# A two-layer graph network: stores issued later than their producers, and the last four norms on VectorE

## The chip, the cores and the metric

The kernel runs on one core of one Trainium2 chip. The metric is the time of one execution on the device in microseconds (us), as the median of several runs. TensorE (PE in the profile) multiplies matrices, with its weight loads listed apart as PEld; VectorE is DVE, ScalarE is ACT, GpSimd is POOL, and SyncE is SP. In this kernel SP issues nearly all transfers between HBM and the on-chip memory SBUF, one after the other.

## The reference

128 batches of a 128 x 512 array x go through two layers, in f32. H is 8 heads, and adj is a 128 x 128 matrix that serves as the mixing matrix of layer 0 and as the attention mask of layer 1.

```python
# layer 0
h = jnp.maximum(_layernorm(x), 0.0)
x = x + (einsum('nm,bmd->bnd', adj, h) @ weight + bias)
# layer 1
h = jnp.maximum(_layernorm(x), 0.0)
q, k, v = heads(h @ w_qkv)
attn = softmax(where(adj == 0, -inf, q @ k.T * scale))
o = (attn @ v) @ w_proj + b_proj
ln = (o - mu) * rsqrt(var + 1e-5) * gamma + beta      # mu, var over the 512 values of a row
x = x + o + ln
```

The change touches the place of many stores in the order of work, and the last three lines for the last four batches.

## The kernel before

The kernel writes its own schedule. While it is built, `put(t, f, *a)` places a piece of work at a planned time t in us in a heap, and the pieces are then emitted in order of t. Each engine runs its own instructions in that order, and each instruction waits on semaphores for what it depends on. So the planned time sets only the order on each engine. SP is one such stream: a transfer that waits for its data holds back all transfers behind it.

```python
    def put(t, f, *a):
        count[0] += 1
        heapq.heappush(later, (t, count[0], f, a))
    ...
    while later:
        t, _, f, a = heapq.heappop(later)
        f(*a)
```

Two transposes are made by a round trip through HBM[...]: `exchange` stores an array to HBM and brings it back with four loads in another order. It serves the normalized input h1 of layer 1 (in the profile d<-h and h<-d) and the softmax probabilities (d<-s and sx<-d). In line numbers, L220 is the store and L225 the loads.

```python
    def exchange(t, b, dst=None):
        w = b.shape[2]
        d = dram.tile([P, Q, w], F32, name=f"d{w}")
        nc.sync.dma_start(out=d, in_=b)                                  # L220
        put(t, exchange_back, b if dst is None else dst, d)

    def exchange_back(dst, d):
        for q in range(Q):
            nc.sync.dma_start(out=dst[q * R:(q + 1) * R, :, :],          # L225
                              in_=d[:, q, :].rearrange("(n r) w -> r n w", n=Q))
```

The result of layer 0 is parked in HBM (x1d) until the end of the batch, and loaded again as x1b (or x, in the last eight batches).

```python
    def keep_x1(i):
        if i >= AHEAD:
            nc.gpsimd.tensor_tensor(X[i], X[i], beta_b, op=ALU.add)      # L335
        X1D[i] = dram.tile([P, D], F32, name="x1d", bufs=20)
        nc.sync.dma_start(out=X1D[i], in_=X.pop(i))                      # L337
```

The softmax of a batch: VectorE adds the mask to the scores (L401) and takes the maximum (L406), ScalarE computes the exponentials (L425), GpSimd divides by the sum (L435). Then comes the exchange, and VectorE transposes the returned blocks (L441) for the attention's matmuls (L450). There are two buffers s for the masked scores and one buffer sx for what returns. Late odd batches (123, 125, 127) have `spare` buffers: the two halves of one free h1T tile, half 0 for the scores and half 1 for what returns.

```python
    def softmax_mask(i, ps):
        s = late(0) if spare(i) else work.tile([P, Q, H * R], F32, name="s", bufs=2)
        ...
            nc.vector.tensor_tensor(s[...], ps[e]..., m4, op=ALU.add)    # L401

    def softmax_divide(i, t, e, sm):
        nc.vector.reciprocal(sm, sm)                                     # L433
        ...
        nc.gpsimd.tensor_tensor(e, e, sm..., op=ALU.mult)                # L435
        S[i] = late(1) if spare(i) else work.tile([P, Q, H * R], F32, name="sx", bufs=1)
        exchange(max(t + 5, read_at(i)), e.rearrange(...), S[i])
```

Products with weights add their parts into PSUM banks; VectorE adds a bank to the result in SBUF (L306 for the first part, L263 for later ones, with pd, pc and pz as the banks), and TensorE reuses the bank after that. For the last four batches the projection is a plain product (L468), and VectorE adds the bias (L663).

The last norm is split over three engines. VectorE computes mean and variance (L201, L202, L204), GpSimd the power -1/2 (L206), VectorE the shift (L211), GpSimd adds o to x1 (L485), ScalarE normalizes (L490), GpSimd multiplies by gamma (L491) and adds (L497; L496 adds beta in the first eight batches only, as the others have it in x1 already). SP stores the output (L498).

```python
    def finish(batches, t):
        shifts, args = stats_of([O[i] for i in batches])
        put(t + 3, shifts)
        for n, (i, arg) in enumerate(zip(batches, args)):
            put(t + 1 + 3 * n, lambda i=i: nc.gpsimd.tensor_tensor(X1B[i], X1B[i], O[i], op=ALU.add))  # L485
            put(t + 3 + 3 * n, finish_out, i, t + 3 + 3 * n, arg)

    def finish_out(i, t, arg):
        n = O.pop(i)
        nc.scalar.activation(n, n, AF.Identity, **arg)                                                 # L490
        put(t + 1.5, lambda: nc.gpsimd.tensor_tensor(n, n, gamma_b, op=ALU.mult))                      # L491
        put(t + 3, finish_last, i, n, X1B.pop(i))

    def finish_last(i, n, x1):
        if i < AHEAD:
            nc.gpsimd.tensor_tensor(n, n, beta_b, op=ALU.add)                                          # L496
        nc.gpsimd.tensor_tensor(n, n, x1, op=ALU.add)                                                  # L497
        nc.sync.dma_start(out=out[i], in_=n)                                                           # L498
```

The constants that matter are AHEAD = 8 (the first batches, with another order), LATE = 120 (the last eight batches, which form the tail with an order of its own) and LAST = 124.

Of the kernel before, what the change touches and what calls it, by code (L numbers as in the profile page):

```python
# [20 lines left out]
def kernel(  # L21
# [30 lines left out]
    nc = tc.nc  # L52
    B, N, D = x.shape
    H = 8
    HD = D // H
    C = D // P
    G = 4
    Q, R = 4, 32
# [5 lines left out]
    work = ctx.enter_context(tc.tile_pool(name="work", bufs=2))  # L64
    stat = ctx.enter_context(tc.tile_pool(name="stat", bufs=8))
# [5 lines left out]
    LATER = []  # L71
    X, H0, YT, X1D, H1, H1T, WQ, QKT, V, S, PT, OT, O, X1B, LEFT0, LEFT1, LEFT2 = ({} for _ in range(17))
# [15 lines left out]
    gamma_b = const.tile([P, D], F32)  # L88
# [74 lines left out]
    minus_half = const.tile([P, 2], F32)  # L163
# [48 lines left out]

        return shifts, [dict(bias=shift[:, n:n + 1], scale=rs[:, n:n + 1]) for n in range(w)]

    def exchange(t, b, dst=None):


        w = b.shape[2]
        d = dram.tile([P, Q, w], F32, name=f"d{w}")
        nc.sync.dma_start(out=d, in_=b)  # L220
        put(t, exchange_back, b if dst is None else dst, d)

    def exchange_back(dst, d):
        for q in range(Q):
# [100 lines left out]
    def norm1_out(i, t, arg):  # L325
        h1 = H1[i] = work.tile([P, Q, C, R], F32, name="h1", bufs=4)
        nc.scalar.activation(h1.rearrange("p q c r -> p c q r"), X[i].rearrange("p (c q r) -> p c q r", c=C, q=Q),
                             AF.Relu, **arg)
        exchange(t + 4.5, h1.rearrange("p q c r -> p q (c r)"))
        put(t + (1.5 if i >= AHEAD else 0), keep_x1, i)  # L330

    def keep_x1(i):

        if i >= AHEAD:
            nc.gpsimd.tensor_tensor(X[i], X[i], beta_b, op=ALU.add)  # L335
        X1D[i] = dram.tile([P, D], F32, name="x1d", bufs=20)
        nc.sync.dma_start(out=X1D[i], in_=X.pop(i))  # L337


    def flip(i):  # L340
# [53 lines left out]
        put(t + 1, softmax_mask, i, ps)  # L394

    def softmax_mask(i, ps):
        s = late(0) if spare(i) else work.tile([P, Q, H * R], F32, name="s", bufs=2)
        s = s.rearrange("p q (h r) -> p h q r", h=H)
        m4 = maskb.rearrange("p (q r) -> p q r", q=Q).unsqueeze(1).to_broadcast([P, C, Q, R])
        for e in range(2):  # L400
            nc.vector.tensor_tensor(s[:, e * C:(e + 1) * C], ps[e].rearrange("p c (q r) -> p c q r", q=Q), m4, op=ALU.add)  # L401
        put(softmax_at(i), softmax_max, i, softmax_at(i), s)
# [6 lines left out]
    def spare(i):  # L409
        return i > LATE + 2 and i % 2  # L410

    def late(n):

        if not LATER:
            t = work.tile([P, C, G, P], F32, name="h1T").rearrange("p (n c) j m -> p n (c j m)", n=2)
            LATER.extend(t[:, n].rearrange("p (q w) -> p q w", q=Q) for n in range(2))
        return LATER[n]

    def softmax_exp(i, t, s, shift):
# [12 lines left out]
    def softmax_divide(i, t, e, sm):  # L432
        nc.vector.reciprocal(sm, sm)  # L433
        e = e.rearrange("p h q r -> p q h r")
        nc.gpsimd.tensor_tensor(e, e, sm.unsqueeze(1).unsqueeze(3).to_broadcast([P, Q, H, R]), op=ALU.mult)  # L435
        S[i] = late(1) if spare(i) else work.tile([P, Q, H * R], F32, name="sx", bufs=1)
        exchange(max(t + 5, read_at(i)), e.rearrange("p q h r -> p q (h r)"), S[i])

    def flip_probs(i):
        PT[i] = work.tile([P, 2 * C, P], F32, name="pT", bufs=2)  # L440
# [44 lines left out]
            put(t + 1 + 3 * n, lambda i=i: nc.gpsimd.tensor_tensor(X1B[i], X1B[i], O[i], op=ALU.add))  # L485
            put(t + 3 + 3 * n, finish_out, i, t + 3 + 3 * n, arg)

    def finish_out(i, t, arg):
        n = O.pop(i)
        nc.scalar.activation(n, n, AF.Identity, **arg)  # L490
        put(t + 1.5, lambda: nc.gpsimd.tensor_tensor(n, n, gamma_b, op=ALU.mult))  # L491
        put(t + 3, finish_last, i, n, X1B.pop(i))

    def finish_last(i, n, x1):
        if i < AHEAD:
            nc.gpsimd.tensor_tensor(n, n, beta_b, op=ALU.add)  # L496
        nc.gpsimd.tensor_tensor(n, n, x1, op=ALU.add)  # L497
        nc.sync.dma_start(out=out[i], in_=n)  # L498

# [8 lines left out]
    BEGIN, LAST, AHEAD = -3, B - G, 8  # L508
# [36 lines left out]
    LATE = LAST - G  # L545
    AT = {key: [] for key in "asQpD"}
    t, last = when(LATE, 0), ""
# [39 lines left out]
    for j in range(B // 2):  # L587
        a, b = 2 * j, 2 * j + 1
        i = a - 8
        if a < AHEAD:  # L590
            t = mix_at(a) - (8.5 if a else 5)
            put(t, norm0, j, t)
            for n in (a, b):
                t = mix_at(n) + 5.2
# [15 lines left out]
        i = a + 5  # L610
        t = attend_at(b) + 2
        if b < LAST:
            put(t, pair_left, j, t, 3.4 if i < LATE else 1.5, OT, LEFT2, "osum")
            n = 7 * (a - LATE + 4) // 2
# [3 lines left out]
        else:  # L618
            ends = []
            for n in (a, b):  # L620
                t = AT["D"][n - LAST]
                put(t, project_whole, n, t)
                ends.append(((n,), t + 4.6))
        for batches, t in ends:
            for n in batches:
                put(t - 7 + 3 * (n % 2), reload, n)
            put(t, finish, batches, t)

    steps = []
# [63 lines left out]
```

## Time and profile before

| What | Value |
| --- | --- |
| median of 3 runs (lowest to highest) | 2372.13 us (2368.23 to 2372.77) |
| span of the profiled execution | 2374.6 us |
| mean granted TensorE clock | 0.996 |
| moved by DMA | 518.86 MB, 218 GB/s in the mean |
| start of the tail (attention of batch 116) | 2243.1 us |
| last matmul ends | 2361.8 us |

The profile shows one execution. For each engine it gives the busy time and its share of the span, and for groups of equal instructions the line, the output and inputs, the count and the mean duration. The waits name the engine and line that waited, and the instruction whose end released it. The chain of waits is followed back from the last instruction, so it shows what each step waited for. The timeline lists single instructions with their start and duration, and in brackets the idle time before them. SPq lines are transfers being issued on SP; they take effect some microseconds later (a store d<-s of 512 KB lands 3.0 us after its issue in the median, a load sx<-d of 128 KB as well).

### The profile page before, as it was taken

Reading aid. Unit: us, or ns where it says so; the run is one execution under the profiler, and the core shown is the slowest. Engines: PE = TensorE matmul, PEld = TensorE weight load, DVE = VectorE, ACT = ScalarE, POOL = GpSimd, SP = SyncE. Lnnn points to the kernel's source line nnn. Section 1 sums busy time; section 2 is a strip of 40 time slices with the busy share of each in tenths; the row PEclk is TensorE's granted clock in tenths of the full one; section 3 lists DMA queues with packets and bytes.
Section 4 is the critical chain, followed back from the end, with each engine's and each line's share of the span. In section 5 each row is a group of like instructions: output and inputs, shape, how many; then the busy total and the mean of one; then the engine's idle time right before and its main releaser. Section 6 shows DMA issues by size and latency. Waiting matters only on the chain.

```text
span 2374.6 us, 43019 instructions
## 1 busy us (share of the span) xinstructions
PE 2332.3 (98%) x14131; PEld 2052.9 (86%) x14131; DVE 1462.2 (62%) x3287; ACT 1066.1 (45%) x3202; POOL 1671.4 (70%) x1592
## 2 busy tenths in 40 slices
PE   8999999999999999999999999999999999999996
PEld 7888888888888888888888888888888888888885
DVE  6556656665665566666666665666666666566654
ACT  3444444454444444444544444444445444444442
POOL 4467777777677766776776777677777767866667
PEclk9999999999999999999999999999999999999998
DMA  7576676766766767677677767677676676676664
GB/s 261 186 221 204 220 231 214 232 222 211 227 218 215 225 211 231 217 220 235 214 216 233 218 217 229 215 227 222 218 232 216 217 233 213 222 229 208 213 209 139
DMA packets 395885, 518.86 MB, mean 218 GB/s; under 512 B 39696, under 2 KB 247696, under 8 KB 395664
## 3 DMA queue, kind: packets, MB, share of 16 engines
q1 hardware_dynamic: 394976, 515.53, 68.7%
q8 instruction: 113, 1.85, 0.3%
q14 instruction: 108, 0.88, 0.1%
q10 hardware_dynamic: 688, 0.59, 0.1%
HBM read 345.05 MB, written 170.92 MB: 217 GB/s over the span
## 4 chain that ended last, share of the span: by engine, by line
PE 83%; DMA 4%; POOL 4%; DVE 4%; ACT 2%; SPq 2%; issue 1%; POOLq 0%; DVEq 0%
PE pc L372 36%; PE pd L300 24%; PE pz L372 6%; PE ps L392 4%; PE pmix L286 4%; PE po L450 4%; PE pz L300 4%; DMA sx<-d 2%; SPq L225 2%; DMA x1b<-x1d 1%; ACT s L425 1%; PE pd L468 1%; POOL x1b L485 1%; DVE pT L441 1%; DVE st L201 1%
## 5 line engine op out<-in xcount | busy, mean ns | idle before, releaser
L206 POOL TENSOR_TENSOR rs<-ve,minus_half 128x2 f32<-128x2 f32 (+1 forms) x194 | 135.6, 699 | 618.0 <-DVE ve L204 617.3
L372 PE MATMUL pc<-hsum,wq 128*128 128x256 f32 x1984 | 468.3, 379 | 3.4 <-POOL o L491 1.8
L372 PEld LDWEIGHTS pc<-hsum,wq 128*128 128x128 f32 x1984 | 376.6, 190 | 55.4 <-POOL o L491 2.2
L425 ACT ACTIVATE s<-s,mx 128x128 f32<-128x128 f32 x1000 | 387.8, 389 | 4.2
L435 POOL TENSOR_TENSOR s<-s,sm 128x1024 f32<-128x1024 f32 x125 | 239.1, 1913 | 38.4 <-DVE sm L433 38.2
L300 PE MATMUL pd<-wp_sb,osum 128*128 128x256 f32 x992 | 254.2, 379 | 1.4 <-DVE sm L433 1.4
L300 PE MATMUL pd<-w_sb,ysum 128*128 128x256 f32 x960 | 246.3, 379 | 0.0
L663 ACT COPY oT<-po 128x512 f32<-128x512 f32 x128 | 74.9, 586 | 372.0 <-PE po L450 372.0
L372 PE MATMUL pc<-wq,hsum 128*128 128x256 f32 x992 | 238.1, 383 | 1.0 <-ACT s L425 1.0
L372 PE MATMUL pc<-h1T,wq 128*128 128x256 f32 x992 | 237.6, 382 | 0.0
L441 DVE STREAM_TRANSPOSE pT<-sx 128x1024 f32<-128x1024 f32 x125 | 155.0, 1240 | 125.0 <-DMA sx<-d 123.0
L372 PEld LDWEIGHTS pc<-wq,hsum 128*128 128x128 f32 x992 | 186.6, 190 | 29.3 <-ACT s L425 1.3
L372 PEld LDWEIGHTS pc<-h1T,wq 128*128 128x128 f32 x992 | 185.9, 190 | 27.9 <-DMA wq<-in_L_gnn_w_qkv_dram 0.3
L306 DVE TENSOR_TENSOR o<-pd,bp_b 128x256 f32<-128x256 f32 x248 | 103.0, 416 | 171.7 <-PE pd L300 171.4
L300 PEld LDWEIGHTS pd<-wp_sb,osum 128*128 128x128 f32 x992 | 184.0, 190 | 24.5 <-issue 1.8
L376 ACT COPY qkT<-pc 128x512 f32<-128x512 f32 x256 | 144.5, 575 | 128.6 <-PE pc L372 128.4
L300 PEld LDWEIGHTS pd<-w_sb,ysum 128*128 128x128 f32 x960 | 177.9, 190 | 21.7
L490 ACT ACTIVATE o<-o,shift,rs 128x512 f32<-128x512 f32 x128 | 103.4, 808 | 196.4 <-POOL osum L234 123.0
L401 DVE TENSOR_TENSOR s<-ps,maskb 128x512 f32<-128x512 f32 x250 | 155.4, 683 | 56.4 <-PE ps L392 55.6
L425 ACT ACTIVATION_READ_ACCUMULATOR s<-s,mx 128x1 f32 x1000 | 187.2, 187 | 0.0
L201 DVE BATCH_NORM_STATS2 st<-x 128x6 f32<-128x512 f32 x256 | 171.9, 672 | 4.4 <-DMA x<-in_x_dram 4.4
L485 POOL TENSOR_TENSOR x1b<-x1b,o 128x512 f32<-128x512 f32 x120 | 152.9, 1275 | 25.7 <-DMA x1b<-x1d 25.2
(141 smaller groups left out, 4691.8 us busy)
## 6 DMA issues: line engine op xcount, KB each, us to landing
wq<-wt SPq DMA_DIRECT2D x372, 256.0 KB, 4.0
wq<-in_L_gnn_w_qkv_dram SPq DMA_DIRECT2D x279, 256.0 KB, 3.7
d<-s SPq DMA_DIRECT2D x125, 512.0 KB, 3.0
sx<-d SPq DMA_DIRECT2D x500, 128.0 KB, 3.0
x<-in_x_dram SPq DMA_DIRECT2D x128, 256.0 KB, 4.5
d<-h SPq DMA_DIRECT2D x128, 256.0 KB, 2.9
x1d<-x SPq DMA_DIRECT2D x128, 256.0 KB, 3.1
h<-d SPq DMA_DIRECT2D x512, 64.0 KB, 2.3
```

Of the source, the lines that this page charges most:

```text
L201: nc.vector.bn_stats(st, src)
L206: nc.gpsimd.tensor_tensor(rs, ve, minus_half[:, :w], op=ALU.pow)
L300: nc.tensor.matmul(p[:, 0, :], lhsT=left[k][:, c, :], rhs=w_sb[:, k, c, :], start=first and c == 0, stop=last and c == 1, skip_group_check ...
L306: nc.vector.tensor_tensor(results[n], p[:, 0, :], addend[n // 2][:, n % 2 * F:(n % 2 + 1) * F], op=ALU.add)
L372: nc.tensor.matmul(p[:, half, :], lhsT=lhsT, rhs=rhs, start=first and half == 0 and c == 0, stop=last and c == 1, skip_group_check=True)
L376: nc.scalar.copy(results[n], p)
L401: nc.vector.tensor_tensor(s[:, e * C:(e + 1) * C], ps[e].rearrange("p c (q r) -> p c q r", q=Q), m4, op=ALU.add)
L425: nc.scalar.activation(s[:, h], s[:, h], AF.Exp, bias=shift[:, h:h + 1], scale=scale, accum_out=sm[:, h:h + 1])
L435: nc.gpsimd.tensor_tensor(e, e, sm.unsqueeze(1).unsqueeze(3).to_broadcast([P, Q, H, R]), op=ALU.mult)
L441: nc.vector.transpose(PT[i].rearrange("p h (q r) -> p q h r", q=Q), S.pop(i).rearrange("p q (h r) -> p q h r", h=H))
L485: put(t + 1 + 3 * n, lambda i=i: nc.gpsimd.tensor_tensor(X1B[i], X1B[i], O[i], op=ALU.add))
L490: nc.scalar.activation(n, n, AF.Identity, **arg)
```

## The change

The aim is that no transfer at the head of SP's stream waits for its producer, and that the last batches leave less work on GpSimd. It has four parts.

- Each store gets its own planned time, some us after the instruction that makes its data: 1.2 us for h1, 2.2 us for the probabilities, 2 us for x1 (where GpSimd still adds beta), 5 us for an output of a batch under 120 and 1.5 us for the others. The loads that bring exchanged data back keep their planned times.
- The store of an x1 without beta and the other stores become pieces of work of their own, so other transfers can be placed between.
- The spare buffers alternate: batch 125 has its scores in one of two free yT tiles and batch 127 in the other, and what returns for them goes to the two halves of the h1T tile.
- For batches 124 to 127 the last norm ends with two VectorE operations, each of which reads two tensors and one value per row: (o - mean) * gamma, then that times the power plus x1. ScalarE's activation, the shift and two GpSimd operations fall away for them.

```diff
-    def exchange(t, b, dst=None):
+    def exchange(t, t_back, b, dst=None):
         w = b.shape[2]
         d = dram.tile([P, Q, w], F32, name=f"d{w}")
-        nc.sync.dma_start(out=d, in_=b)
-        put(t, exchange_back, b if dst is None else dst, d)
+        put(t, nc.sync.dma_start, d, b)
+        put(t_back, exchange_back, b if dst is None else dst, d)
 ...
-        exchange(t + 4.5, h1.rearrange("p q c r -> p q (c r)"))
-        put(t + (1.5 if i >= AHEAD else 0), keep_x1, i)
+        exchange(t + 1.2, t + 4.5, h1.rearrange("p q c r -> p q (c r)"))
+        t += 1.5 if i >= AHEAD else 0
+        put(t, keep_x1, i, t)
 ...
-        nc.sync.dma_start(out=X1D[i], in_=X.pop(i))
+        put(t + (2 if i >= AHEAD else 0), nc.sync.dma_start, X1D[i], X.pop(i))
 ...
-        s = late(0) if spare(i) else work.tile([P, Q, H * R], F32, name="s", bufs=2)
+        s = late((i - LATE - 1) // 2 * (i > LATE + 3)) if spare(i) else work.tile([P, Q, H * R], F32, name="s", bufs=2)
 ...
+        if n > 1 and len(LATER) == 2:
+            LATER.extend(work.tile([P, C, 2, P], F32, name="yT").rearrange("p c j m -> p c (j m)") for _ in range(2))
         return LATER[n]
 ...
-        S[i] = late(1) if spare(i) else work.tile([P, Q, H * R], F32, name="sx", bufs=1)
-        exchange(max(t + 5, read_at(i)), e.rearrange("p q h r -> p q (h r)"), S[i])
+        S[i] = late((i - LATE - 1) // 2 % 2) if spare(i) else work.tile([P, Q, H * R], F32, name="sx", bufs=1)
+        exchange(t + 2.2, max(t + 5, read_at(i)), e.rearrange("p q h r -> p q (h r)"), S[i])
 ...
+    def finish_end(i, t):
+        nc.gpsimd.tensor_tensor(X1B[i], X1B[i], O[i], op=ALU.add)
+        st = stat.tile([P, nc.vector.BN_STATS_DIM], F32, name="st")
+        nc.vector.bn_stats(st, O[i])
+        ...  # mean and variance mv, ve = variance + EPS
+        nc.gpsimd.tensor_tensor(rs, ve, minus_half[:, :1], op=ALU.pow)
+        n = work.tile([P, D], F32, name="h0", bufs=2)
+        nc.vector.scalar_tensor_tensor(n, O.pop(i), mv[:, 0:1], gamma_b, op0=ALU.subtract, op1=ALU.mult)
+        put(t + 1.9, end_last, i, n, rs)
+
+    def end_last(i, n, rs):
+        nc.vector.scalar_tensor_tensor(n, n, rs, X1B.pop(i), op0=ALU.mult, op1=ALU.add)
+        nc.sync.dma_start(out=out[i], in_=n)
 ...
-        put(t + 3, finish_last, i, n, X1B.pop(i))
+        put(t + 3, finish_last, i, t + 3, n, X1B.pop(i))
 ...
-        nc.sync.dma_start(out=out[i], in_=n)
+        put(t + (5 if i < LATE else 1.5), nc.sync.dma_start, out[i], n)
 ...
-            put(t, finish, batches, t)
+            if a < LAST:
+                put(t, finish, batches, t)
+            else:
+                put(t, finish_end, batches[0], t)
```

More of the change, by code (lines that the diff above doesn't have):

```diff
@@ L328, in norm1_out, with keep_x1 @@
                              AF.Relu, **arg)
-        exchange(t + 4.5, h1.rearrange("p q c r -> p q (c r)"))
-        put(t + (1.5 if i >= AHEAD else 0), keep_x1, i)
-    def keep_x1(i):
+        exchange(t + 1.2, t + 4.5, h1.rearrange("p q c r -> p q (c r)"))
+        t += 1.5 if i >= AHEAD else 0
+        put(t, keep_x1, i, t)
+    def keep_x1(i, t):
         if i >= AHEAD:
@@ L486, in finish @@
             put(t + 3 + 3 * n, finish_out, i, t + 3 + 3 * n, arg)
+    def finish_end(i, t):
+        nc.gpsimd.tensor_tensor(X1B[i], X1B[i], O[i], op=ALU.add)
+        st = stat.tile([P, nc.vector.BN_STATS_DIM], F32, name="st")
+        nc.vector.bn_stats(st, O[i])
+        mv = stat.tile([P, 2, nc.vector.BN_AGGR_DIM], F32, name="mv")[:, 0]
+        nc.vector.bn_aggr(mv, st)
+        ve = stat.tile([P, 2], F32, name="ve")[:, :1]
+        nc.vector.tensor_scalar(ve, mv[:, 1:2], EPS, None, op0=ALU.add)
+        rs = stat.tile([P, 2], F32, name="rs")[:, :1]
+        nc.gpsimd.tensor_tensor(rs, ve, minus_half[:, :1], op=ALU.pow)
[5 more added lines that the diff above has]
+        nc.sync.dma_start(out=out[i], in_=n)
     def finish_out(i, t, arg):
@@ L491, in finish_out, with finish_last @@
         put(t + 1.5, lambda: nc.gpsimd.tensor_tensor(n, n, gamma_b, op=ALU.mult))
-        put(t + 3, finish_last, i, n, X1B.pop(i))
-    def finish_last(i, n, x1):
+        put(t + 3, finish_last, i, t + 3, n, X1B.pop(i))
+    def finish_last(i, t, n, x1):
         if i < AHEAD:
```

## The prediction

> **What bounds the kernel now.** I read the engines' shares first, then the waits of TensorE, then those of the DMA queue (SP), then the chain of work into one of TensorE's gaps, and last the timeline of the end.
>
> ```profile
> PE 2332.3 (98%) x14131; PEld 2052.9 (86%) x14131; DVE 1462.2 (62%) x3287; ACT 1066.1 (45%) x3202; POOL 1671.4 (70%) x1592
> ```
>
> TensorE is the bound: 2374.6 - 2332.3 leaves 42.3 us in which it is not busy, and no matmul is removed or reordered (the order of instructions on TensorE is the same in both kernels). The change can only win some of these 42.3 us and the slow matmuls that follow a long gap. So which wait ends each gap? Columns of the waits: total us, times, longest.
>
> ```profile
> PE pd L300 <- DVE x L263: 9.9, 11, 1.9
> PE po L450 <- DVE pT L441: 3.5, 1, 3.5
> PE pd L300 <- DVE o L263: 3.4, 1, 3.4
> ...
> PE pc L372 <- POOL o L491: 1.8, 1, 1.8
> PE pd L300 <- DVE sm L433: 1.4, 1, 1.4
> ```
>
> By window, the first line lies wholly between 100 and 2243 us (4.5 up to 700, 3.7 up to 1400, 1.8 after): it is the steady part. The four others lie after 2243, in the tail. After the last matmul (2361.8 us) another 12.8 us pass. The DMA queue waits far longer, and in order:
>
> ```profile
> SPq L498 <- POOL o L497: 304.8, 123, 8.2
> SPq L220 <- POOL s L435: 225.9, 123, 21.7
> ```
>
> L498 is the store of an output, L220 the store of a batch's probabilities. What such a wait does to others shows in the chain into the 1.81 us gap at 304.76 (start, us, what):
>
> ```profile
> 295.82 1.28 POOL o L497
> 297.12 0.34 SPq L498
> ...
> 297.88 0.32 SPq L225
> ...
> 299.22 3.25 DMA sx<-d
> ...
> 302.55 1.25 DVE pT L441
> 303.80 0.58 DVE v L263
> 304.38 0.34 DVE x L263
> 304.76 1.13 PE pd L300 x4
> ```
>
> The load of sx (probabilities coming back, L225) sits in the SP stream behind an output store, which waits for GpSimd's last addition. The load starts late, VectorE stands 4.33 us before the transpose, and the addition that frees TensorE's PSUM bank is late. I looked at the gaps at 230, 590, 741, 814, 888, 1540 and 2191 too: in each one the output store is issued right after a GpSimd L497 and the sx load 0.4 us later.
>
> **What the Trainium skill says.** *Perfetto Trace Analysis*, section Sequencer Loop: an engine reads instructions one by one and each waits for its semaphores. The trace agrees for SP: nothing behind L498 is issued while it waits (at most 8.2 us). *SBUF — State Buffer*, Who interferes with whom: a VectorE instruction with two SBUF inputs and a GpSimd instruction that reads SBUF exclude each other for the whole instruction. The trace agrees: a VectorE subtraction of two SBUF tensors took 1.54 us at 31.71 while GpSimd added until 32.70, and 0.64 to 0.69 alone. *Vector Engine (DVE) Microarchitecture Reference*, Points that are easy to get wrong: a scalar-tensor-tensor with two non-bf16 SBUF sources runs at half throughput. No such instruction is in this trace. *TensorE: Matmul & The Clock Gate*, What's actually happening: TensorE's clock falls after an idle window of about 3.4 us. The trace agrees: after the 3.4 us gap the next four matmuls take 2.07 us, not 1.03, and the following eight 2.38, not 1.89.
>
> **The change part by part.**
>
> *Output stores 5 us later (batches under 120).* In the order of SP's instructions the odd batch's four sx loads and the weight load after them now stand ahead of the output store. What then holds the sx load is the weight load before it and the previous transpose, since there is one sx buffer. At 2182.64 the output store ended its wait and the sx load came at 2183.07; the weight load before was out at 2177.76 and the transpose ended at 2180.28 (2179.04 + 1.23). So the load moves from 2183.07 to about 2180.3, 2.8 us. In the same way it moves from 297.88 to about 292.6 (transpose 291.28 + 1.24), 5.3 us, and from 879.68 to about 876.4, 3.2 us. The longest gaps are 1.9, 1.8 and 1.7 us, each below its shift. **9.9 us go, and 0.1 each[...] (1.13 us for four matmuls, not 1.03): together 10 us**, with 8 to 11 as my range.
>
> *h1, probability and x1 stores 1 to 2 us later.* They wait less at the head of the queue. In some places a weight load, which itself waits for TensorE, now stands ahead of them (0.57 us at 1442.68). The returns h<-d start after x1d in both kernels. I give it 0, plus or minus 1 us. In the first 100 us TensorE's gaps come from GpSimd and ScalarE, whose order does not change: 0.
>
> *Other buffers for the masked scores of batches 125 and 127.* Before, all odd late batches share one half of an h1T tile:
>
> ```profile
> 2321.83 1.29 DVE L401 TENSOR_TENSOR h1T<-ps,maskb 128x512 f32<-128x512 f32 x2 [4.89 <-DMA d<-h1T]
> 2324.63 2.07 PE L300 MATMUL pd<-wp_sb,oT 128*128 128x256 f32 x4 [3.40 <-DVE o L263]
> ```
>
> The mask of 127 waits 4.89 us until the probabilities of 125 are stored, VectorE stands, and TensorE loses 3.40 us plus 1.04 and 0.49 of slow matmuls. With its own buffer the mask follows its scores, some 4.3 us sooner (2317.5). I then walk the order of VectorE: the transpose of 124 needs its load (issued until 2318.03, landing some 3.6 us later: 2321.7, not 2324.8), so the maximum of 127 comes at about 2323.7 and not 2327.08, 3.4 us sooner. The rest of 127 (exponentials, division, store, load, transpose) keeps that lead. In SP's new order one output store stands ahead of 127's store, which costs about 1.6 us there, but the load of 127 formerly stood behind the same two output stores (issued 2342.14, though its data was stored at about 2340.5), so its lead at the load is still 3.5. TensorE now arrives earlier too, and waits for this transpose again: the 3.5 us gap at 2348.66 stays, perhaps 4.8 long. **3.5 us go**; the gaps of 1.8 and 1.4 us, at 2275 and 2281, follow from order on ScalarE and from one sx buffer, and stay.
>
> *The norm of the last four batches.* Removed from GpSimd: the gamma multiplication and the last addition, 8 x 1.26 = 10.1 us; from ScalarE 4 x 0.81 us; from VectorE four small shifts of 0.20. Added on VectorE: 8 operations over 128x512.
>
> ```profile
> 2361.81 0.69 DVE L663 TENSOR_TENSOR o<-pd,bp_b 128x512 f32<-128x512 f32 x1 [1.57 <-PE pd L468]
> ...
> 2363.49 0.15 DVE L204 TENSOR_SCALAR ve<-mv 128x1 f32<-128x1 f32 x1
> 2363.55 1.26 POOL L497 TENSOR_TENSOR o<-o,x 128x512 f32<-128x512 f32 x1
> ...
> 2370.41 1.26 POOL L497 TENSOR_TENSOR o<-o,x 128x512 f32<-128x512 f32 x1
> ```
>
> Before, statistics are ready at 2363.64, but GpSimd works through its queue until 2371.67, and the store ends 2.9 us later. After,[...] each operation takes 0.69 us as the other two-tensor ones do: first 2363.64 to 2364.35; GpSimd's x+o 2362.5 to 2363.8 and the power 0.55 to 2364.4; second to 2365.1; plus 2.9 is 2368.0, so 6.6 us less. With the mutual exclusion the order x+o, power, first, second costs 0.7 in this batch, and VectorE's cycle of 4.0 us per batch exceeds the 3.46 of TensorE, so that three batches push another 1.1: 4.8 less. At half throughput (1.2 us each, an estimate from the page and the 0.69) the cycle is 4.4, and about 3.5 less remain. **I take 5.**
>
> Sum: 10 + 3.5 + 5 = 18.5, so 2372.1 - 18.5 = **2353.5 us**.
>
> **The rivals.** (1) *Another wait takes the place of the removed one*: sx has one buffer, x1b still lands late (GpSimd waited 25.2 us for it in all), and stores now queue behind weight loads that wait for TensorE. Then only half of the 10 us would come: about 2358.5. Against it: the shifts exceed every gap, and DVE's order has the same slack as before. (2) *VectorE becomes the bound of the end*, by half throughput or by the exclusion: the end gains 2 to 3.5, about 2356. For it speaks the page, against it that tensor-tensor with two f32 SBUF inputs runs at 0.69. (3) *The gain is larger*: if the softmax of 127 is no longer waited for, its 3.5 us gap goes as well, and with the full 6.6 at the end about 2348. Against it: its chain is long and moves only with its mask. (4) *Later stores hold buffers longer*: the s buffer of an odd batch is stored about 2 us later; if the next mask waits, VectorE stalls in every pair, 60 times 0.5 us would eat everything: about 2372. The trace shows the odd store at 1440.97 and the next masks from 1451.48, so 10 us stand against a delay of 2 and a landing of 3.0 (median of these stores).
>
> **Range and chances.** Steady part 7 to 11, tail 2 to 5, end 3 to 6.6: 12 to 22.6 as extremes, 2349.5 to 2360. With the runs' own spread (2368.2 to 2372.8) and something I overlook, 2346 to 2361 for 8 in 10. A gain of 2% would be 47 us, more than the whole idle time of TensorE: 0.01. A loss of 2% needs rival 4 at full strength: 0.01.
>
> **What would show it.** In the steady part: TensorE's wait for DVE x L263 (9.9 us) near 0, VectorE's wait for sx (123.0 us) far down, SP's wait at the output store near 0. In the tail: no idle time before the mask of 127, and still a gap of 3 to 5 us before the last attention. At the end: the two new operations at 0.7 or at 1.2 us, and 6 to 9 us from last matmul to end, not 12.8. I am wrong if TensorE gets waits for weights or for GpSimd's sums that it doesn't have now, or if the sx loads stay as late as they are.

## The result, and the profile after

The changed kernel takes **2350.99 us** (median of 4 runs, 2350.07 to 2351.88), beside 2371.10 us for the kernel before in the same comparison (4 runs, 2368.23 to 2372.77). The ratio is 0.9916, 95% interval 0.9899 to 0.9934: 20.1 us less. Predicted were 2353.5 us, a gain of 18.5, in a range of 2346 to 2361. One caution for all that follows: the profile of before belongs to an execution of 2376.43 us, 4 to 5 us above its median.

In the new kernel every piece of work that was put into the heap carries the line of the loop that takes it out, so L689 stands for all stores that are now given out late. The engines first, from the page of the kernel after:

```profile
PE 2327.0 (99%) x14131; PEld 2053.7 (87%) x14131; DVE 1479.7 (63%) x3291; ACT 1062.5 (45%) x3198; POOL 1662.3 (71%) x1584
```

Span 2349.0 less 2327.0 leaves 22.0 us in which TensorE is not busy; it was 42.3. Its largest waits (total us, times, longest):

```profile
PE po L454 <- DVE pT L445: 4.1, 1, 4.1
PE pc L373 <- POOL hsum L234: 3.7, 2, 2.1
PE pc L373 <- ACT qkT L377: 2.9, 1, 2.9
PE pc L373 <- POOL osum L234: 1.8, 1, 1.8
...
PE pd L300 <- DVE sm L437: 0.3, 1, 0.3
```

There is no line "DVE x" any more (9.9 us before) and no "DVE o L263" (3.4). The wait for the last transpose grew from 3.5 to 4.1. The queue of SP, in the same view:

```profile
SPq L689 <- POOL s L439: 301.0, 98, 18.4
...
SPq L689 <- ACT h L327: 184.3, 88, 3.8
SPq L225 <- DVE pT L445: 124.1, 60, 2.1
...
SPq L689 <- POOL o L520: 7.8, 8, 2.9
```

The wait at the output store went from 304.8 to 7.8 us. The aim that no store waits for its producer is not reached, though: SP now waits longer at the probability stores (301.0 us, 225.9 before) and at the h1 stores (184.3, 137.7 before). The sx load (L225) now waits for the transpose that empties the one sx buffer; what is left of its wait for the probabilities to be stored is 89.6 us (164.4 before). VectorE's wait for sx was 123.0 us in 61 places and is now:

```profile
DVE pT L445 <- DMA sx<-d: 5.9, 3, 4.5
```

The timeline of SP, VectorE and GpSimd in the steady part shows the new order (start, us, engine, line):

```profile
866.51 1.23 DVE L445 STREAM_TRANSPOSE pT<-sx 128x1024 f32<-128x1024 f32 x1
...
867.77 1.74 SPq L225 DMA_DIRECT2D sx<-d  x4
...
868.90 1.27 POOL L520 TENSOR_TENSOR o<-o,x1b 128x512 f32<-128x512 f32 x1
...
869.61 0.38 SPq L159 DMA_DIRECT2D wq<-wt  x1
...
870.20 0.36 SPq L689 DMA_DIRECT2D out_dram<-o  x1
```

The load leaves 0.03 us after the transpose has ended (866.51 + 1.23), while the addition that the output store needs has not begun.

By stretches of the two profiled executions: up to the tail's first matmuls (batch 116) 14.4 us were won (2243.12 to 2228.70); from there to the end of the last matmul 5.6 (118.7 to 113.0); from the last matmul to the end 5.5 (12.8 to 7.3). The first figure contains the unlucky execution of before, so the timed gain is smaller than the three together. Between the third attention (209.82 us) and the start of the tail TensorE is listed as busy for the whole 2018.88 us.

### The profile page after: what moved, and what is told of

It reads as the page before. It is cut to its first block, busy times and chain, and to the rows that moved or that the text cites. A ratio compares the mean times of both kernels' runs of the same rounds, so it can differ in the third digit from the quotient of the medians.

```text
span 2349.0 us, 43086 instructions
## 1 busy us (share of the span) xinstructions
PE 2327.0 (99%) x14131; PEld 2053.7 (87%) x14131; DVE 1479.7 (63%) x3291; ACT 1062.5 (45%) x3198; POOL 1662.3 (71%) x1584
## 4 chain that ended last, share of the span: by engine, by line
PE 94%; DMA 2%; POOL 1%; issue 1%; DVE 1%; SPq 0%; ACT 0%; POOLq 0%; DVEq 0%
PE pc L373 42%; PE pd L300 26%; PE pz L373 7%; PE ps L393 5%; PE po L454 5%; PE pmix L286 4%; PE pz L300 4%; POOL rs L206 0%; DMA sx<-d 0%; DMA x<-in_x_dram 0%; DMA oT<-in_L_gnn_w_qkv_dram 0%; DMA sx<-in_L_gnn_w_qkv_dram 0%; POOL hsum L234 0%; DVE pT L445 0%; SPq L225 0%
## 5 line engine op out<-in xcount | busy, mean ns | idle before, releaser
L206 POOL TENSOR_TENSOR rs<-ve,minus_half 128x2 f32<-128x2 f32 x190 | 133.5, 702 | 619.5 <-DVE ve L204 613.0
L689 ACT COPY oT<-po 128x512 f32<-128x512 f32 x128 | 74.8, 585 | 371.0 <-PE po L454 371.0
L377 ACT COPY v<-pc 128x512 f32<-128x512 f32 x128 | 74.3, 581 | 214.6 <-PE pc L373 214.6
L277 POOL TENSOR_TENSOR x<-x,b_b 128x512 f32<-128x512 f32 x128 | 161.8, 1265 | 2.4 <-DMA h<-d 2.4
```

What stands on the lines that cost most here:

```text
L206: nc.gpsimd.tensor_tensor(rs, ve, minus_half[:, :w], op=ALU.pow)
L277: nc.gpsimd.tensor_tensor(x_, x_, b0_b, op=ALU.add)
L377: nc.scalar.copy(results[n], p)
```

## The experiments

The runs came in three groups, each on one chip with its own runs of before: A (before 2371.76 us, 37 runs), B (2376.52 us, 9 runs) and C (2374.51 us, 17 runs). A gain is the difference of the two medians. The ratio uses all runs, so it can say a little more or less than the medians do; it has its 95% interval in brackets.

**Theory at the start**: the steady gain is the output store alone, which no longer stands ahead of the sx load; the tail and the end have their own parts; the other stores do nothing. **Rivals**: the other stores carry part of it; another wait takes the place; the end is limited by VectorE.

### The four parts, each alone (group A)

Output stores late, the rest as before:

```diff
-        nc.sync.dma_start(out=out[i], in_=n)
+        put(t + (5 if i < LATE else 1.5), nc.sync.dma_start, out[i], n)
```

> Kernel before with only the output stores given out later (5 us for batches under 120, 1.5 us for the rest). My theory: all of the steady part's gain is this store alone, since the load of the returning probabilities (sx) no longer stands behind it: TensorE's wait for the addition x on VectorE goes from 9.9 us to under 0.5, the queue's wait at the output store from 304.8 us to under 20, VectorE's wait for sx from 123 to under 15; time some 10 to 13 us below before, about 2359 to 2361; tail and end as before (last matmul to span end 12.8 us, a 3.4 us wait at the mask of batch 127). Rival A, the gain needs the other stores (h1, x1, probabilities) to be later too: only about half, some 2365. Rival B, another wait takes its place: the waits go, the time stays within 3 us of before.

Measured: 2364.80 us, 7.0 less, ratio 0.9970 (0.9958 to 0.9983); runs from 2361.87 to 2366.07. The waits are nearly as expected: no wait for x, VectorE's wait for sx 6.9 us, the wait at the output store 28.1 (expected under 20), the tail unchanged. But the median is the one that rival A names (2365), not that of the theory. What is left are waits of TensorE for weights of 1.2 us in all. The profile is that of the fastest of these six executions, 9.9 us below the median of before and close to the theory's 2359 to 2361, so it doesn't show what the slower ones lose.

Other buffers for the scores of batches 125 and 127, nothing else:

```diff
-        s = late(0) if spare(i) else work.tile(...)
+        s = late((i - LATE - 1) // 2 * (i > LATE + 3)) if spare(i) else work.tile(...)
-        S[i] = late(1) if spare(i) else work.tile(...)
+        S[i] = late((i - LATE - 1) // 2 % 2) if spare(i) else work.tile(...)
```

> Kernel before with only the spare buffers of the masked scores of batches 125 and 127. My theory: the 4.9 us wait of the mask of 127 and TensorE's 3.4 us gap behind it go, with 1.5 us of slow matmuls, and nothing in the steady part: 3 to 5 us below before, about 2367; the gap before the last attention stays 3 to 4.1 us; the 1.4 us gap near 2281 stays if it came from the other changes, and goes to about 0.3 if the buffers alone removed it. Rival: the gain before the last attention is lost again because the softmax of 127 isn't limited by its mask, then under 1 us.

Measured: 2366.69 us, 5.1 less, ratio 0.9979 (0.9970 to 0.9987). The mask of 127 in its timeline:

```profile
2311.45 1.29 DVE L401 TENSOR_TENSOR yT<-ps,maskb 128x512 f32<-128x512 f32 x2 [0.47 <-PE ps L392]
```

It follows its scores after 0.47 us (4.89 before), TensorE's 3.4 us gap is gone, and the wait before the last attention is 4.1. The 1.4 us gap near 2281 is 0.6 here, but 0.3 in the kernel with only the output stores late and 0.8 in that with only the new end, neither of which touches these buffers: its size differs from run to run, and the expectation about it tells nothing.

The new end for the last four batches, nothing else:

```diff
-            put(t, finish, batches, t)
+            if a < LAST:
+                put(t, finish, batches, t)
+            else:
+                put(t, finish_end, batches[0], t)
```

> Kernel before with only the last norm of the last four batches in two VectorE operations. My theory: last matmul to span end falls from 12.8 to 7.0 to 8 us, the two operations 0.7 to 0.85 us each when nothing excludes them: 5 us below before, about 2366. Rival A, two f32 SBUF sources at half throughput: operations of 1.2 us and 3.5 us below. Rival B, the queue of VectorE also delays the tail's other work: under 3 us below, with longer TensorE waits for o of VectorE after 2335 us.

Measured: 2367.35 us, 4.4 less (5.5 by the ratio), ratio 0.9977 (0.9968 to 0.9987). The last batch's two operations, and one of an earlier batch, in its timeline:

```profile
2347.70 1.75 DVE L504 SCALAR_TENSOR_TENSOR h<-h,rs,x 128x512 f32<-128x512 f32 x1 [0.45 <-POOL rs L498]
...
2360.26 0.84 DVE L500 SCALAR_TENSOR_TENSOR h<-o,mv,gamma_b 128x512 f32<-128x512 f32 x1
2361.54 0.75 DVE L504 SCALAR_TENSOR_TENSOR h<-h,rs,x 128x512 f32<-128x512 f32 x1 [0.44 <-POOL rs L498]
```

0.75 to 0.84 us, not 1.2: rival A falls. From the last matmul to the end are 8.8 us, more than the 7 to 8 expected: for one batch (at 2354.18) VectorE stands 1.71 us for GpSimd's power, which comes after GpSimd's additions for earlier batches.

The other stores late (h1 1.2 us, x1 2, probabilities 2.2 for batches under 120), the output stores at once:

```diff
-        nc.sync.dma_start(out=d, in_=b)
-        put(t, exchange_back, b if dst is None else dst, d)
+        put(t, nc.sync.dma_start, d, b)
+        put(t_back, exchange_back, b if dst is None else dst, d)
...
-        nc.sync.dma_start(out=X1D[i], in_=X.pop(i))
+        put(t + (2 if i >= AHEAD else 0), nc.sync.dma_start, X1D[i], X.pop(i))
```

The later probability stores of the last batches were left out here: with one pair of spare halves for all of them, as in before, the order of work would let the data be overwritten before they are stored. So the alternating buffers would also be what permits the later stores there; no run shows it.

> Kernel before with only the other stores later (h1 1.2 us, x1 2 us, probabilities 2.2 us for batches under 120), output stores at once as before. My theory: 0 plus or minus 1 us, TensorE's wait for x on VectorE stays at 8 to 11 us and the queue's wait at the output store stays near 300 us. Rival A: these stores carry part of the gain, 3 to 6 us below before. Rival B: they hold buffers longer and cost 2 to 5 us, hidden in the whole change by the other parts.

Measured: 2367.65 us, **4.1 less**, ratio 0.9982 (0.9975 to 0.9988). My theory said 0; rival A is right. But the expected signs of the theory also fail: TensorE's wait for x is 5.1 us, not 8 to 11, while the wait at the output store stays at 286.5.

The four parts add up: 7.0 + 5.1 + 4.4 + 4.1 = 20.6, beside 20.1 for the whole. Each gain has an interval of 1.5 to 3 us on either side, so that they meet to half a microsecond is in part chance.

### Does the wait of 9.9 us belong to the kernel? What do the other stores do? (group B)

> Kernel before once more, for a second profile of it. In the first profile (2376.4 us, 4.7 above the median of 37 runs) TensorE waited 9.9 us for the addition x on VectorE, and the kernels with only the spare buffers or only the end changed, whose steady part is that of before, 7.2 and 5.2. If that wait is a quantity that differs from run to run: 5 to 8 us at a time near 2371. If 9.9 is its usual size: 9 to 11 here too, and the 7.2 and 5.2 came from the changes.

Measured: 2380.41 us in this one execution, 10.6 us of wait for x in 16 places, and 125.7 us of VectorE's wait for sx. So 9.9 is no upper outlier of all executions. But this group's before is 4.8 us slower in the median than group A's, and on chip A the kernels with the same steady part showed 7.2 and 5.2. The wait differs by chip and by execution; this one profile of a slower chip can't part the two expectations cleanly.

The whole change, but the other stores at once as in before:

```diff
-        put(t, nc.sync.dma_start, d, b)
-        put(t_back, exchange_back, b if dst is None else dst, d)
+        nc.sync.dma_start(out=d, in_=b)
+        put(t, exchange_back, b if dst is None else dst, d)
```

(with x1's store at once too)

> Kernel after, but with the h1, x1 and probability stores at once as in before; output stores late, spare buffers and new end kept. The single parts gained 7.0 (output stores), 5.1 (spare buffers), 4.4 (end) and 4.1 us (other stores), 20.6 together, against about 20 for the whole. If the parts add up: 3 to 5 us above after, 2354 to 2356, with a weight load that comes late now and then. If the other stores only relieve the same waits that the late output store removes already (my first theory): within 1 us of after, 2350 to 2352.

Measured: 2356.58 us (2353.24 to 2357.98), ratio to before 0.9918 (0.9904 to 0.9931). That is 5.6 above the kernel after, slightly more than expected, but on another chip than after's first runs; the ranges don't meet. TensorE's waits in its profile have what after lacks:

```profile
PE pc L372 <- POOL x1b L487: 2.3, 1, 2.3
...
PE pz L372 <- DMA wq<-in_L_gnn_w_qkv_dram: 1.2, 1, 1.2
...
PE pc L372 <- DMA wq<-in_L_gnn_w_qkv_dram: 0.9, 2, 0.5
PE pc L372 <- DMA wq<-wt: 0.5, 1, 0.5
```

So once the output store is out of the way, the next store that waits in the queue (SP waits 421.8 us for s in this kernel) can make a weight load late now and then; that this store is the cause was not followed in single gaps. The waits for weights are 2.6 us in all. Most of the loss lies in the tail: the profiled execution is 3.9 us longer than that of after, of which 3.5 pass between the tail's first attention and the last matmul (116.5 and 113.0 us), and 0.7 in the steady part. Apart from the first profile of before, TensorE waits for a weight load in every profiled execution whose other stores are not all late (0.3 to 2.6 us in all), and in none of the four in which they are.

The probability stores alone 2.2 us late:

```diff
-        nc.sync.dma_start(out=d, in_=b)
+        if store is None:
+            nc.sync.dma_start(out=d, in_=b)
+        else:
+            put(store, nc.sync.dma_start, d, b)
...
-        exchange(max(t + 5, read_at(i)), e.rearrange(...), S[i])
+        exchange(max(t + 5, read_at(i)), e.rearrange(...), S[i], t + 2.2 if i < LATE else None)
```

> Kernel before with only the probability stores 2.2 us later (batches under 120); h1, x1 and output stores at once. If the 4.1 us of all the other stores come from the queue's wait for GpSimd's probabilities (225.9 us in all): 3 to 4 us below before, about 2368. If they come from the h1 and x1 stores: within 1 us of before.

Measured: 2434.86 us, **58 us slower**, ratio 1.0249 (1.0231 to 1.0267). Neither expectation. SP's timeline says what became of the order (in before it was d<-h, d<-s, d<-h, x1d, wq, x1d, h<-d):

```profile
1448.54 1.51 SPq L221 DMA_DIRECT2D d<-h  x2
1451.44 0.32 SPq L340 DMA_DIRECT2D x1d<-x  x1
1451.86 0.38 SPq L159 DMA_DIRECT2D wq<-wt  x1
1453.90 0.32 SPq L340 DMA_DIRECT2D x1d<-x  x1
1454.27 0.42 SPq L666 DMA_DIRECT2D d<-s  x1
1454.79 4.33 SPq L228 DMA_DIRECT2D h<-d  x8
1459.21 0.40 SPq L159 DMA_DIRECT2D wq<-in_L_gnn_w_qkv_dram  x1
1459.65 0.47 SPq L482 DMA_DIRECT2D x1b<-x1d  x1
```

The probability store, alone moved, fell behind both x1 stores and now stands right ahead of the h loads and of x1b. GpSimd's wait for x1b is 78.1 us (25.2 in before), and TensorE's wait for x 52.6 us in 37 places (9.9 in 11).

Output stores 2.5 us late instead of 5, the rest as before (`5 if i < LATE else 1.5` becomes `2.5 if i < LATE else 0`):

> Kernel before with only the output stores later, by 2.5 us instead of 5 (none for batches from 120 on). In the queue's order this already puts the sx loads of the odd batches ahead of the output store. Theory, only the order of these two counts: the same as with 5 us, 2362 to 2366, TensorE's wait for x under 0.5 us, VectorE's wait for sx under 15. Rival, the length of the delay counts: half the gain, some 2368.

Measured: 2363.84 us (2362.28 to 2364.52), ratio 0.9949 (0.9936 to 0.9961), no wait for x, 7.3 us for sx. The odd batch's load now stands ahead of the output store:

```profile
1447.13 1.74 SPq L225 DMA_DIRECT2D sx<-d  x4
1449.29 0.34 SPq L159 DMA_DIRECT2D wq<-wt  x1
1449.73 0.37 SPq L663 DMA_DIRECT2D out_dram<-o  x1
```

The time is that with 5 us on chip A (2364.80), though before differs by 4.8 us between the two chips. So 2.5 us do what 5 us do; and what the output store costs differs between the chips: 7.0 us on A, 12.7 on B.

### Order or delay, and a version that is better than both (group C)

> Kernel after once more, beside kernel before on the same chip as the next three. Before differs between chips (median 2371.8 on one, 2376.5 on another), and the excess is wait for sx. If after has no such wait left, its time doesn't depend on the chip: 2350 to 2352, and the ratio to before is 0.990 to 0.9915 as before itself comes out.

Measured: 2351.07 us (2349.84 to 2351.27), ratio 0.9904 (0.9891 to 0.9918). The time of after is the same on a second chip where before is 3.4 us slower than in the first comparison.

Output stores 1 us late (`1 if i < LATE else 0`); the store then still stands ahead of the odd batch's sx load:

> Kernel before with the output stores only 1 us later (none from batch 120 on). In the queue's order a store then still stands ahead of the odd batch's sx load; it only changes places with a probability store. Theory, only the order of output store and sx load counts: same as before within 1.5 us, TensorE's wait for x 5 to 11 us, VectorE's wait for sx over 95. Rival, every microsecond of delay helps: 3 to 6 us below before.

Measured: 2373.49 us, ratio 1.0000 (0.9991 to 1.0009). No gain at all: TensorE waits 8.0 us for x in 12 places, VectorE 115.4 us for sx, and the same two transfers stand as in before:

```profile
1452.89 0.34 SPq L663 DMA_DIRECT2D out_dram<-o  x1
1453.32 1.83 SPq L225 DMA_DIRECT2D sx<-d  x4
```

With the 2.5 us of the run above this is a step and not a slope: **what counts among these delays is the order of output store and sx load.**

h1 and x1 stores late, probability and output stores at once:

```diff
-        exchange(t + 4.5, h1.rearrange("p q c r -> p q (c r)"))
+        exchange(t + 4.5, h1.rearrange("p q c r -> p q (c r)"), store=t + 1.2)
...
-        nc.sync.dma_start(out=X1D[i], in_=X.pop(i))
+        put(t + (2 if i >= AHEAD else 0), nc.sync.dma_start, X1D[i], X.pop(i))
```

> Kernel before with only the h1 stores 1.2 us and the x1 stores 2 us later; probability and output stores at once. New theory for the 4.1 us of all the other stores: with x1 later the half of the h1 loads and the x1b loads stand ahead of one x1 store or behind less, x1b lands sooner, GpSimd's wait for x1b falls from 25 us to under 12 (it was 7.2 with all other stores late, and 78 with the probability stores alone late), so GpSimd's last addition, the output store and the sx load behind it are sooner: 2 to 5 us below before. Rival, it takes all three stores together to keep their order: x1b wait 25 or more, same as before or slower.

Measured: 2419.48 us, **45 us slower**, ratio 1.0192 (1.0174 to 1.0211). The rival is right: these stores help only together. SP's timeline:

```profile
1464.28 0.32 SPq L221 DMA_DIRECT2D d<-s  x1
1464.69 0.39 SPq L667 DMA_DIRECT2D d<-h  x1
1465.17 0.74 SPq L159 DMA_DIRECT2D wq<-in_L_gnn_w_qkv_dram  x1
1466.01 0.63 SPq L667 DMA_DIRECT2D d<-h  x1
```

Both h1 stores now stand behind the probability store, which waits for GpSimd (376.4 us in all); h<-d, and x1b behind it, come later.

To see whether x1b is the link, I took from the traces how long after GpSimd's last addition to an x1 (that of beta) the loads of x1b leave (median of some 115 loads between 100 and 2240 us), beside the waits:

| Kernel | x1b load leaves after | GpSimd's wait for x1b | SP's wait at the output store | TensorE's wait for x | time against before |
| --- | --- | --- | --- | --- | --- |
| all other stores late | 4.99 us | 7.2 us | 286.5 us | 5.1 us | -4.1 us |
| before | 6.08 | 25.2 | 304.8 | 9.9 | 0 |
| h1 and x1 stores late | 6.39 | 55.8 | 341.2 | 39.0 | +45.0 |
| probability stores late | 6.97 | 78.1 | 360.5 | 52.6 | +58.3 |

All five columns rise together. The chain that fits is: x1b later, GpSimd's last addition later, output store later, sx load behind it later, TensorE stands. The run without the other late stores supports it: there GpSimd waits 25.3 us for x1b as in before, but since the output store no longer stands ahead of the sx load, VectorE waits only 7.5 us for sx.

For the two losses the chain is well supported, though no run changed the landing of x1b alone. For the gain of 4.1 us it is not shown beyond its first links, because the row of before is one execution above its median. The kernel with only the new end has the steady part of before and ran on the chip of the first row: its x1b loads leave after 6.07 us and GpSimd waits 15.9 us for x1b, but it waits 282.1 us at the output store and 5.2 for x, no more than with all other stores late. What the gain consists of after x1b stays open.

The version after these readings: the kernel after, with the output stores 5 us late in the tail too.

```diff
-        put(t + (5 if i < LATE else 1.5), nc.sync.dma_start, out[i], n)
+        put(t + 5, nc.sync.dma_start, out[i], n)
```

> Kernel after with the output stores 5 us late in the tail as well (it was 1.5 us for batches from 120 on). Theory: the probability store of batch 127 no longer stands behind an output store (in after it was issued at 2318.91, GpSimd's division had ended at 2317.26), so its load, the transpose and the last attention come 1.5 us earlier: the last wait of TensorE for the transpose from 4.1 to about 2.6 us, time 1 to 2 us below after. Rival, the load of 127 waits for something else, or the last output stores end later: same as after within 0.5 us.

Measured: **2348.37 us** (2347.92 to 2349.52), ratio to before 0.9895 (0.9881 to 0.9908), 2.7 below after on the same chip, and the ranges don't overlap. In after, SP's timeline has an output store ahead of 127's probabilities:

```profile
2318.51 0.36 SPq L689 DMA_DIRECT2D out_dram<-o  x1
2318.91 0.43 SPq L689 DMA_DIRECT2D d<-yT  x1
2319.39 0.45 SPq L483 DMA_DIRECT2D x<-x1d  x1
2321.09 0.34 SPq L689 DMA_DIRECT2D out_dram<-o  x1
2322.12 1.74 SPq L225 DMA_DIRECT2D h1T<-d  x4
```

In the new version they stand behind its load:

```profile
2317.02 0.34 SPq L689 DMA_DIRECT2D d<-yT  x1
2317.40 1.23 SPq L483 DMA_DIRECT2D x<-x1d  x1
2320.24 1.74 SPq L225 DMA_DIRECT2D h1T<-d  x4
2322.09 0.85 SPq L689 DMA_DIRECT2D out_dram<-o  x2
```

The load leaves 1.9 us earlier, of which 0.8 is an earlier start of the tail in this execution. The last attention of after, then of the new version:

```profile
2328.45 1.91 PE L454 MATMUL po<-pT,v 128*64 128x128 f32 x16 [4.11 <-DVE pT L445]
```

```profile
2326.07 1.09 PE L454 MATMUL po<-pT,v 128*64 128x128 f32 x16 [2.28 <-DVE pT L445]
```

The span is 3.0 us shorter than that of after on this chip (2346.5 and 2349.5): the tail 3.8 less, the end 1.5 more, all before the tail 0.7 less. Of the tail's share 2.3 us are the shorter wait before the last attention, most of the rest matmuls that no longer run slowly after it. The 0.7 lies wholly in the first 210 us, where the wait for qkT is 1.2 us here and 2.9 in both executions of after, whose order there is the same; I take it as chance, so some 2 us are the edit's own.

The stages of the profiled executions, in us, put the parts side by side. The steady stretch runs from the third attention to the first of the tail, the tail to the last matmul:

| Kernel (group) | up to the third attention | steady | tail | end |
| --- | --- | --- | --- | --- |
| before (first comparison) | 210.9 | 2032.3 | 118.7 | 12.8 |
| before (B) | 209.7 | 2036.1 | 120.1 | 12.6 |
| output stores 1 us late (C) | 209.3 | 2031.0 | 117.5 | 12.8 |
| other score buffers only (A) | 208.7 | 2029.3 | 114.3 | 12.6 |
| new end only (A) | 211.2 | 2029.0 | 116.3 | 8.8 |
| other stores late only (A) | 209.4 | 2025.5 | 118.5 | 12.6 |
| output stores late only (A) | 209.3 | 2019.3 | 118.8 | 12.7 |
| output stores 2.5 us late only (B) | 211.2 | 2019.5 | 118.4 | 12.9 |
| all but the other stores (B) | 209.5 | 2019.6 | 116.5 | 7.3 |
| after (first comparison) | 209.8 | 2018.9 | 113.0 | 7.3 |
| after (C) | 209.7 | 2018.9 | 113.6 | 7.3 |
| after, tail stores 5 us late (C) | 209.0 | 2018.9 | 109.9 | 8.8 |

On chip A the output stores alone shorten the steady stretch by 9.7 to 10.0 us, and leave 0.4 for the other stores, which alone take 3.6 to 3.8 off it. So in the steady stretch these two parts win the same time, not separate times; in the one profile of the change without the other stores, most of what is lost lies in the tail.

## Why the prediction was right, point by point

- **Output stores, 10 us: right mechanism, with luck in the number.** The order of SP's instructions did what was predicted: the sx load moved ahead, bounded by the previous transpose, and the wait for x went to nothing. On chip A the steady stretch is 9.7 to 10.0 us shorter. But 9.9 us was read from one execution above the median; in the kernels whose sx load still stands behind the output store and whose other stores were not moved the wait is 9.9, 10.6, 8.0, 7.2 and 5.2. On chip A it is only 5.2 and 7.2: the rest of the gain is time in which matmuls are listed as busy for longer (2022.3 us in before's steady stretch, 2018.9 in after's), which the prediction left out apart from its 0.1 us per gap. Its sum is also off by one: 9.9 and eleven times 0.1 make 11.0. The medians value the part at 7.0 us on chip A and 12.7 on B.
- **Other stores, 0 plus or minus 1: wrong.** This is the step that failed. Alone they give 4.1 us, and without them the change is some 5.6 us slower. I had looked at what moves in front of the h loads and found nothing that moves TensorE at once. What I missed is that x1b leaves a microsecond sooner (4.99 against 6.08), and that without these delays TensorE waits for weights now and then and the tail takes 3.5 us more in the one profile; how the earlier x1b becomes time stays open. That the stores wait less at the head of the queue was wrong too: of the three only the x1 stores do (48.6 us, 53.2 before). The table's last two rows show how near a large loss lay: the same delays on a part of the stores cost 45 and 58 us.
- **Tail, 3.5: too small, 5.1 alone and 5.6 in the profile.** The mask went as worked out (0.46 us of idle time before it), and one output store ahead of 127's probabilities does cost: taking it away gave 2.7 us, some 2 of them its own (1.6 predicted). The prediction's own terms are 3.40 us of gap and 1.04 and 0.49 of slow matmuls, less 1.3 for a longer wait before 127's attention, 3.6 in all. Three things were off, which make the 3.6 into 5.6. The second group of slow matmuls takes 2.58 us in the trace of before, not the 2.38 that was read, so 0.69 was lost and not 0.49. The wait before 127's attention grew to 4.1 only, where I had allowed for 4.8. And the gap near 2281, which I said stays, was 0.3 and not 1.4, by chance of the run as it seems.
- **End, 5: right.** 5.5 in the profile; alone 4.4 by the medians and 5.5 by the ratio. The two operations take 0.84 and 0.75 us:

```profile
2342.27 0.68 DVE L689 TENSOR_TENSOR o<-pd,bp_b 128x512 f32<-128x512 f32 x1
...
2343.03 1.26 POOL L494 TENSOR_TENSOR x<-x,o 128x512 f32<-128x512 f32 x1 [1.47 <-DVE o L689]
...
2344.00 0.84 DVE L504 SCALAR_TENSOR_TENSOR h<-o,mv,gamma_b 128x512 f32<-128x512 f32 x1
2344.25 0.99 POOL L502 TENSOR_TENSOR rs<-ve,minus_half 128x1 f32<-128x1 f32 x1
2345.28 0.75 DVE L508 SCALAR_TENSOR_TENSOR h<-h,rs,x 128x512 f32<-128x512 f32 x1 [0.44 <-POOL rs L502]
```

  The exclusion came as feared: the power, 0.55 us alone, takes 0.99 and ends 0.40 after the first operation, which it overlaps; the second then starts 0.44 late. So a batch takes 3.7 us on VectorE (2341.60 to 2345.28), less than the 4.0 I feared. The half throughput that the Trainium skill states (*Vector Engine (DVE) Microarchitecture Reference*, Points that are easy to get wrong) is not seen here: 0.75 against 0.68 to 0.69 for a plain addition of the same size.
- **The rivals.** (1) Another wait in place of the removed one: in the whole change no; without the other late stores yes, for weights, 2.6 us in all. (2) VectorE as the bound of the end: in after hardly, as its last bias addition starts 0.5 us after the last matmul. In the version with the later tail stores TensorE comes sooner and the addition starts 2.0 us after it (2339.74, matmuls until 2337.72): there 8.8 us follow, not 7.3, which takes back part of the gain. As in the kernel with only the new end, VectorE had stood for GpSimd's power before (1.68 us at 2335.39). (3) The gap of 127 vanishes: no. (4) Later stores hold the s buffers: no (its 60 times 0.5 us would have been 30, more than the whole gain), but a part of the late stores did cost far more than anything else here.
- **The sum**: 18.5 predicted, 20.1 measured. The missing 4.1 of the other stores and 1.6 of the tail were mostly made up by an output store part of 7.0 and an end of 4.4 (all medians of group A). The total was closer than its terms, which is luck.

## What to carry to other kernels

When one queue issues all transfers, ask of each instruction in it what it waits for and which urgent load stands behind it: a store moved by 1 us gave nothing, by 2.5 us all, since its place relative to one load mattered. Read such an order after each edit, and move stores as a group: the same delay on some of them lost 45 and 58 us where all together won 4. These three runs had the output store in its old place; no run tried a part of the group with the output store late, so how large the loss is then is open. And take the size of a stall from several executions, and from the length of a whole stage and not from the listed waits alone: a wait for landings differs by chip and by run, and here removing it also removed that spread (a steady stretch of 2029 to 2036 us became 2018.9 in each of three executions).

## What the runs showed of the hardware

- The kernel before had medians of 2371.8, 2376.5 and 2374.5 us on three chips; the kernel after 2351.0 and 2351.1 in two comparisons. In the profiled executions the difference lies in the steady stretch, which was 2029.0 to 2036.1 us long with the sx load behind the output store (2025.5 with the other stores late), and 2018.9 to 2019.6 on every chip with it ahead.
- A scalar-tensor-tensor operation over 128 x 512 in f32 took 0.75 us alone and 1.75 us beside a GpSimd addition (at 2347.70 in the kernel with the new end only); a GpSimd power over 128 x 1 took 0.55 alone and 0.99 beside a VectorE operation with two SBUF tensors.
- After a gap of 4.11 us sixteen attention matmuls took 1.91 us, after 2.28 us 1.09. The idle window of about 3.4 us that the Trainium skill gives (*TensorE: Matmul & The Clock Gate*, What's actually happening) fits these two, but it is no sharp limit on the gap that a trace lists, and the length alone does not decide. Before the last attention of all kernels, gaps of 2.18 to 2.87 us were followed by the fast 1.09, and gaps of 3.12, 3.33 and 4.56 us by 1.70, 1.45 and 1.73. With only the other stores late, a gap of 3.64 us cost nothing beyond its length: four matmuls in 1.13 us and eight in 1.89, with a granted clock of 1.00, where 3.40 us in before were followed by 2.07 and 2.58.

```profile
2315.46 1.13 PE L300 MATMUL pd<-wp_sb,oT 128*128 128x256 f32 x4 [3.64 <-DVE o L263]
2316.43 1.89 PE L373 MATMUL pc<-wq,hsum 128*128 128x256 f32 x8
```
